# Four banks that keep a tile's attention sums, its new values in one go, and value matmuls on both sides of the transposes

## The chip, the cores and the metric

The kernel runs on one core of a Trainium2 chip. The metric is the device time of one execution in microseconds, lower being better. Before the change it is 2471.74 us, the median of three runs between 2467.19 and 2473.27.

## The reference

Four residual layers are applied one after another to x, which holds 64 batch rows of 32 tokens with 512 features. The time around the change is that of the third layer, attention over a paged cache:

```python
x = x + L0(x)      # per-condition 32x32 mixing of the 32 rows
x = x + L1(x)      # dense 512x512 plus a rank-16 adapter
x = x + L2(x)      # attention, below
x = x + L3(x)      # as L0, other weights

def L2(x):
    q, k, v = x @ Wq.T, x @ Wk.T, x @ Wv.T       # 32 query heads, 8 key/value heads, 128 wide
    q, k = rope(rmsnorm(q, q_norm_w)), rope(rmsnorm(k, k_norm_w))
    k_all = concat(k_cache[block_table], k)      # 512 cached and 32 new keys per batch row
    v_all = concat(v_cache[block_table], v)
    scores = q @ k_all.T * SCALE                 # masked by the cached length
    return (softmax(scores) @ v_all) @ Wo.T
```

All numbers are float32.

## The kernel before

**Tiles, steps, units, slots.** The 2048 tokens form 16 tiles of 128 tokens; a tile holds four batch rows (`NB` = 4). Key/value heads are taken in two groups of four (`KG` = 4), so there are 32 steps of one group and one tile. A step has four units, one for each batch row `j`, and a unit has four heads `k`. One unit and one head make a slot: 512 slots, 16 to a step. Four query heads share a key/value head, so a slot's queries are 4 x 32 = 128 rows.

**What a slot does.** The program order is written out by hand in `slot(i)`, and each engine keeps it. `scores` (L832) multiplies the queries with 544 keys in two matmuls (L838, L841) into a tile of two PSUM banks; VectorE (DVE) adds the mask and takes the row minimum (L846), and ScalarE (ACT) takes the exponential (L857). `divide` (L859) takes the reciprocal of the sum on DVE (L862) and scales on ACT: the 512 cached keys' part (L863) and the 32 new keys' part (L864). Two slots later (`LAG`) `flip` (L877) transposes the 128x512 probabilities with four transposes (L880) into the bank of the tag "t", and DVE copies them out (L882). Three slots later (`VLAG`) `values` (L884) adds four chunks of 128 cached keys into the output sum (L893).

A float32 matmul on TensorE appears in the profile as two passes, a transpose as one.

**New keys.** The 32 new keys of four heads are together 128 rows. `flip_new` (L866) transposes them for a whole unit with one transpose (L873) and ACT copies it out (L875). After the fourth head `values_new` (L901) multiplies each head's 32 rows with the 32 rows of its new values (L905): four small matmuls in four row strips of the array, each into its head's sum. `finish` (L913) then copies the unit's four sums to SBUF with two ACT copies (L919, L922), and after the fourth unit `store` (L927, L929) writes the tile's 1 MB to DRAM, on the SP queue but for the last three steps.

**PSUM.** There are eight banks: two for the scores, one "t", one "m" for projections, three for the sums of heads 0 to 2, and one, "o3", which the sum of head 3 shares in turn with the transposes of the rotated heads (`Norm.turn`, L750) and of the cache pages (`Turn.turn`, L266). ACT copies those transposes out in `keep` (L758, L768, and L278, L283).

**Work beside it.** While attention runs, the next two tiles' projections are made, spread over the slots: one or two halves of a projection matmul in nearly every slot (`project`, L643, L651), DVE additions that combine them (`take`, L667, L663), squares on ACT (`squares`, L702, L707), the power on GpSimd (POOL; `power`, L711), and four norm and rotation pieces on DVE (`scale`, `straight`, `swapped`, `sum`) that `norm_piece` (L950) hands out where a slot has room. The slot after the last piece gets the head's transposes; slots in which head 3's sum is being made are passed over.

**Transfers.** `Unit` loads a unit's 16 key pages from SP (L794), `fetch_values` gathers its four chunks of cached values from POOL (L105), `fetch_new` loads the new values from SP (L816), a slot ahead and with two buffers. After attention, the output products (L1323) and the last mixing follow.

Of the kernel before, what the change touches and what calls it, by code (L numbers as in the profile page):

```python
# [27 lines left out]
F32 = mybir.dt.float32  # L28
# [15 lines left out]
P = 128  # L44
B, S, HID = 64, 32, 512
NT = B * S // P
NB = P // S
NC = HID // P
D = 128
# [28 lines left out]
def resid_kernel(  # L78
# [149 lines left out]
    with ExitStack() as l2:  # L228
# [20 lines left out]
        class Turn:  # L249
# [16 lines left out]
            def turn(self):  # L266
                if self.g:
                    self.ps = room["o"].tile([P, HID], F32, name="pageT_ps", tag="o3")
                else:
                    self.ps = ps_s.tile([P, 2 * HID], F32, name="s_ps")  # L270
                for k in range(KG):
                    nc.tensor.transpose(
                        self.ps[:, k * P : (k + 1) * P],
                        self.rows[:, k // 2, (k % 2) * D : (k % 2 + 1) * D],
                        ident,
                    )
# [420 lines left out]
        class Norm:  # L697
# [52 lines left out]
            def turn(self):  # L750
                if "o" in room:
                    self.tp = room["o"].tile([P, REP, P], F32, name="head_ps", tag="o3")
                else:
                    self.tp = ps_t.tile([P, REP, P], F32, name="head_ps", tag="t")
                for h in range(REP):
                    nc.tensor.transpose(self.tp[:, h, :], self.a[:, h, :], ident)  # L756
# [16 lines left out]
        class Unit:  # L773
# [39 lines left out]
            def fetch_new(self):  # L813

                self.v_new = room["v"].tile([P, D], F32, name="v_new", bufs=2)
                nc.sync.dma_start(  # L816
                    out=self.v_new,
                    in_=vn_dram[self.g][self.t][self.j * S : (self.j + 1) * S, :].rearrange(
                        "s (k d) -> k s d", k=KG
                    ),  # L820
                )

            def begin(self):
# [6 lines left out]
                self.sm, self.total, self.pT, self.o_ps = {}, {}, {}, {}  # L830
# [35 lines left out]
            def flip_new(self):  # L866
# [7 lines left out]
                self.pT_new = room["attn"].tile([P, P], F32, name="pT_new", bufs=1)  # L874
# [9 lines left out]
            def values(self, k):  # L884


                if k == 0:
                    self.o_three = room["o"].tile([P, KG - 1, HID], F32, name="o_ps", tag="o")
                    self.o_ps = {i: self.o_three[:, i, :P] for i in range(KG - 1)}
                elif k == KG - 1:  # L890
                    self.o_ps[k] = room["o"].tile([P, HID], F32, name="o_ps3", tag="o3")[:, :P]
                for c in range(NC):
                    nc.tensor.matmul(  # L893
                        self.o_ps[k],
                        lhsT=self.v[c][:, k * D : (k + 1) * D],
                        rhs=self.pT[k][:, c, :],
                        start=(c == 0),
                        stop=False,
                    )

            def values_new(self):  # L901

                for k in range(KG):
                    rows_k = slice(k * S, (k + 1) * S)
                    nc.tensor.matmul(  # L905
                        self.o_ps[k],
# [3 lines left out]
                        stop=True,  # L910
                    )

            def finish(self):  # L913
                if self.j == 0:
                    oT_of[self.s] = room["attn"].tile([P, KG * REP, P], F32, name="oT", bufs=1)
                dst = oT_of[self.s].rearrange("p (k h) s -> p k h s", k=KG)[
                    :, :, :, self.j * S : (self.j + 1) * S
                ]
                nc.scalar.copy(  # L919
                    dst[:, KG - 1], self.o_ps[KG - 1].rearrange("p (h s) -> p h s", h=REP)  # L920
                )
                nc.scalar.copy(  # L922
                    dst[:, : KG - 1],
                    self.o_three[:, :, :P].rearrange("p k (h s) -> p k h s", h=REP),
                )
# [19 lines left out]
        oT_of, rot_of = {}, {}  # L945
# [4 lines left out]
        def norm_piece(slot):  # L950
# [242 lines left out]
        def slot(i):  # L1193
# [14 lines left out]
            if LAG <= i < n + LAG and (i - LAG) % KG == KG - 1:  # L1208
                turned.flip_new()
            run(i, "turn")  # L1210
            if i >= VLAG:
                old = unit_of[(i - VLAG) // KG]
                old.values((i - VLAG) % KG)
                if (i - VLAG) % KG == KG - 1:
                    old.values_new()
                    at(i, "act", old.finish)
                    if old.j == NB - 1:
                        at(i + 1, "store", old.store)
            if new:
                new.divide(k)  # L1220
# [278 lines left out]
```

## Time and profile before

| | |
|---|---|
| median of three runs | 2471.74 us |
| profiled execution, its own time | 2473.52 us |
| span of that execution | 2471.8 us |
| mean granted TensorE clock | 0.999 |
| busy: PE, DVE, ACT, POOL | 2438.3, 1609.2, 1398.3, 1174.2 us |
| attention slots (from the first to the last scores) | 191.2 to 2078.2 us of the span |
| PE busy in the attention slots | 1878.07 of 1887.00 us |

PE is the matmul engine and PEld its weight loads. A group of instructions is named by its line in the kernel, its engine, its operation, and its tiles as out<-in. In a timeline, neighbouring instructions of one group are one row: where it starts, how long it lasts from its first start to its last end, and how many there are. Matmuls overlap at their ends[...]; so the time that a group takes on TensorE is read from its start to the start of the next group.

### The profile page before, as it was taken

The page shows a single profiled execution, that of the slowest core. Times are in us where ns is not written, and L with a number is a line of the kernel's source. Part 1 is how long each engine was busy: PE and PEld are TensorE (multiplying, and loading weights), DVE is VectorE, ACT ScalarE, POOL GpSimd, SP SyncE. Part 2 cuts the span into 40 slices and gives each one's busy share as a digit, 9 for nine tenths or more (in the row PEclk, how much of TensorE's full clock was granted, in tenths as well). Part 3 has the DMA queues.
Part 4 walks back from the last instruction along what each step waited for, and adds up shares of the span by engine and source line. Part 5 has one row for each costly group of instructions (what it writes and reads, how often), then busy time and mean ns, then how long its engine had stood idle before and what let it go on. Part 6 is the DMA issues. An engine that isn't in the chain of part 4 may idle for free.

```text
span 2471.8 us, 47357 instructions
## 1 busy us (share of the span) xinstructions
PE 2438.3 (99%) x13760; PEld 1855.4 (75%) x13760; DVE 1609.2 (65%) x3602; ACT 1398.3 (57%) x4135; POOL 1174.2 (48%) x1096
## 2 busy tenths in 40 slices
PE   7999999999999999999999999999999999999999
PEld 4556777777777777777777777777777788888887
DVE  5767767676767677777777777777776756433222
ACT  2236767676767767677777777777676754000000
POOL 4436555455555565655556555555555753000000
PEclk9999999999999999999999999999999999999999
DMA  7876666666667677756666666565667784333221
GB/s 237 293 231 199 188 198 191 193 195 189 202 188 209 188 218 220 250 180 194 178 189 176 185 179 186 171 192 173 187 178 220 252 258 155 117 112 129 86 86 60
DMA packets 448545, 459.19 MB, mean 186 GB/s; under 512 B 51424, under 2 KB 379488, under 8 KB 440480
## 3 DMA queue, kind: packets, MB, share of 16 engines
q1 hardware_dynamic: 398384, 291.24, 38.1%
q0 software_dynamic: 49904, 164.93, 22.2%
q8 instruction: 112, 1.84, 0.3%
q14 instruction: 145, 1.19, 0.2%
HBM read 384.66 MB, written 79.69 MB: 188 GB/s over the span
## 4 chain that ended last, share of the span: by engine, by line
PE 95%; DMA 2%; issue 2%; SPq 1%; DVE 0%; POOL 0%; ACT 0%; DVEq 0%; POOLq 0%; ACTq 0%
PE proj_ps L651 23%; PE o_ps L893 18%; PE out_ps L1323 15%; PE s_ps L838 11%; PE s_ps L841 9%; PE pT_ps L880 9%; PE l_ps L490 3%; PE head_ps L756 3%; PE o_ps L905 2%; DMA kT<-kT 1%; PE h_ps L474 1%; SPq L794 1%; PE s_ps L873 1%; PE mix_ps L1341 1%; PE mix_ps L435 1%
## 5 line engine op out<-in xcount | busy, mean ns | idle before, releaser
L105 POOL DMA_INDIRECT v_sb<-v,v_rows x512 | 538.1, 1051 | 352.7 <-PE o_ps L893 242.8
L846 DVE CUSTOM_DVE_ANT_0 sm<-s_ps,pen 128x544 f32<-128x544 f32 x512 | 370.9, 724 | 457.9 <-PE s_ps L841 337.2
L893 PEld LDWEIGHTS o_ps<-pT,v_sb 128*128 128x128 f32 x4096 | 519.2, 192 | 133.6 <-issue 126.3
L857 ACT ACTIVATE sm<-sm,top 128x544 f32<-128x544 f32 x512 | 381.8, 746 | 339.6 <-DVE top L846 266.2
L893 PE MATMUL o_ps<-pT,v_sb 128*128 128x128 f32 x4096 | 541.4, 275 | 2.5 <-issue 1.3
L863 ACT ACTIVATE sm<-sm,share 128x512 f32<-128x512 f32 x512 | 369.8, 722 | 175.9 <-DVE share L862 144.2
L882 DVE COPY pT<-pT_ps 128x512 f32<-128x512 f32 x512 | 351.5, 687 | 8.0 <-PE pT_ps L880 4.1
L838 PE MATMUL s_ps<-kT,qT 128*128 128x288 f32 x1024 | 347.0, 420 | 2.8 <-DMA kT<-kT 2.1
L880 PE MATMUL pT_ps<-ident,sm 128*128 128x128 f32 x2048 | 307.7, 273 | 0.6 <-DVE pT L882 0.6
L841 PE MATMUL s_ps<-kT,qT 128*128 128x256 f32 x1024 | 305.3, 380 | 2.4 <-DMA kT<-kT 2.4
L880 PEld LDWEIGHTS pT_ps<-ident,sm 128*128 128x128 f32 x2048 | 256.1, 141 | 52.5 <-DVE pT L882 1.0
L809 POOL TENSOR_SCALAR pen<-key_f,seq_f 128x544 f32<-128x544 f32 x128 | 285.0, 2227 | 11.6 <-issue 0.3
L712 POOL TENSOR_SCALAR ss<-ss 128x4 f32<-128x4 f32 x160 | 56.4, 353 | 438.1 <-ACT sq L707 437.5
L841 PEld LDWEIGHTS s_ps<-kT,qT 128*128 128x128 f32 x1024 | 194.4, 190 | 57.2 <-issue 2.0
L663 DVE TENSOR_TENSOR raw<-proj_ps,raw 128x512 f32<-128x512 f32 x332 | 223.4, 685 | 18.7 <-PE proj_ps L651 13.9
L707 ACT ACTIVATE sq<-raw 128x128 f32<-128x128 f32 x640 | 197.2, 308 | 18.5 <-DVE raw L663 2.3
L714 POOL TENSOR_TENSOR rstd<-ss,minus_half 128x4 f32<-128x4 f32 x160 | 185.1, 1157 | 13.4
L1373 ACT COPY p<-out_ps 128x256 f32<-128x256 f32 x7 | 2.6, 373 | 333.1 <-PE out_ps L1323 333.1
L651 PE MATMUL proj_ps<-sum,x 128*128 128x512 f32 x380 | 186.9, 594 | 0.0
L105 POOL DMA_INDIRECT mix_rows<-in_w,cond_rows x32 | 33.0, 1031 | 309.3 <-DVE mix_diag L171 299.5
L838 PEld LDWEIGHTS s_ps<-kT,qT 128*128 128x128 f32 x1024 | 154.7, 191 | 20.0 <-issue 3.5
L1323 PE MATMUL out_ps<-w,o_in 128*128 128x256 f32 x768 | 167.1, 379 | 0.0
(175 smaller groups left out, 3492.7 us busy)
## 6 DMA issues: line engine op xcount, KB each, us to landing
kT<-kT SPq DMA_DIRECT2D x2048, 64.0 KB
o<-oT SPq DMA_DIRECT2D x29, 1024.0 KB
o_in<-o SPq DMA_DIRECT2D x28, 1024.0 KB
page_rows<-in_kv_cache SPq DMA_DIRECT2D x32, 256.0 KB
v<-in_kv_cache SPq DMA_DIRECT2D x32, 256.0 KB
kT<-page_rows SPq DMA_DIRECT2D x32, 256.0 KB
vn<-raw SPq DMA_DIRECT2D x32, 256.0 KB
v_sb<-v,v_rows POOLq DMA_INDIRECT x512
```

The lines of the kernel that those rows point to most:

```text
L105: nc.gpsimd.indirect_dma_start(out=dst, out_offset=None, in_=table, in_offset=bass.IndirectOffsetOnAxis(ap=index, axis=0),)
L651: nc.tensor.matmul(self.ps, lhsT=self.pair.x[x][:, c if x == "b" else half.start + c, :], rhs=blocks(self.b)[w][:, c, :], start=(c == 0), ...
L809: nc.gpsimd.tensor_scalar(self.pen, key_f, seq_f[:, self.b : self.b + 1], BIG, ALU.is_ge, ALU.mult)
L838: nc.tensor.matmul(ps[:, first:HID], lhsT=q, rhs=self.kT[:, :n1, k, :], start=True, stop=True)
L841: nc.tensor.matmul(ps[:, HID : first + LA], lhsT=q, rhs=self.kT[:, n1:, k, :], start=True, stop=True)
L846: nc.vector.tensor_tensor_reduce(out=sm, in0=ps[:, first : first + LA], in1=self.pen, scale=1.0, scalar=3e38, op0=ALU.add, op1=ALU.min, ac ...
L857: nc.scalar.activation(sm, sm, AF.Exp, bias=top, scale=-1.0, accum_out=total)
L863: nc.scalar.activation(sm[:, :L], sm[:, :L], AF.Copy, scale=share)
L880: nc.tensor.transpose(ps[:, c, :], self.sm[k][:, c * P : (c + 1) * P], ident)
L882: nc.vector.tensor_copy(pT, ps)
L893: nc.tensor.matmul(self.o_ps[k], lhsT=self.v[c][:, k * D : (k + 1) * D], rhs=self.pT[k][:, c, :], start=(c == 0), stop=False,)
L1323: nc.tensor.matmul(ps[:, :HALF], lhsT=o[:, i, :], rhs=w[i // REP][:, i % REP, :], start=(i == 0), stop=(i == KG * REP - 1),)
```

## The change

The four heads' sums of a whole tile stay in four banks, one for each head, with the four units side by side in 128 columns each; only the first matmul into a bank has the start flag. The new values of the four units are added together after the tile's last slot. Four copies, one for each head, take the sums out, two in that slot and two in the next, and each head's 256 KB is stored by itself, heads 0 and 1 from SP and heads 2 and 3 from POOL. In a slot the value matmuls come right after the scores: two chunks, then the probabilities' transposes, then the other two chunks. `flip_new` and `divide` move ahead of the projections. Head and page transposes use the bank "t". The output buffer `oT` has three parts of a quarter tile, `v_new` and `pT_new` have four buffers, `v_new` is loaded early in its tile, and the cached values are gathered one slot earlier. A diff, cut to its core:

```diff
 # Turn.turn
-                    self.ps = room["o"].tile([P, HID], F32, name="pageT_ps", tag="o3")
+                    self.ps = ps_t.tile([P, HID], F32, name="pageT_ps", tag="t")
 # Norm.turn
-                if "o" in room:
-                    self.tp = room["o"].tile([P, REP, P], F32, name="head_ps", tag="o3")
-                else:
-                    self.tp = ps_t.tile([P, REP, P], F32, name="head_ps", tag="t")
+                self.tp = ps_t.tile([P, REP, P], F32, name="head_ps", tag="t")
 # Unit
-                self.v_new = room["v"].tile([P, D], F32, name="v_new", bufs=2)
+                self.v_new = room["v"].tile([P, D], F32, name="v_new", bufs=NB)
-                self.pT_new = room["attn"].tile([P, P], F32, name="pT_new", bufs=1)
+                self.pT_new = room["attn"].tile([P, P], F32, name="pT_new", bufs=NB)
-            def values(self, k):
-                if k == 0:
-                    self.o_three = room["o"].tile([P, KG - 1, HID], F32, name="o_ps", tag="o")
-                    self.o_ps = {i: self.o_three[:, i, :P] for i in range(KG - 1)}
-                elif k == KG - 1:
-                    self.o_ps[k] = room["o"].tile([P, HID], F32, name="o_ps3", tag="o3")[:, :P]
-                for c in range(NC):
+            def values(self, k, chunks):
+                if self.j == 0 and chunks[0] == 0:
+                    o_of[self.s, k] = room["o"].tile([P, NB, P], F32, name="o_ps", tag=f"o{k}")
+                for c in chunks:
                     nc.tensor.matmul(
-                        self.o_ps[k],
+                        o_of[self.s, k][:, self.j, :],
                         lhsT=self.v[c][:, k * D : (k + 1) * D],
                         rhs=self.pT[k][:, c, :],
-                        start=(c == 0),
+                        start=(self.j == 0 and c == 0),
                         stop=False,
+                        skip_group_check=True,
                     )
 # values_new
-                        self.o_ps[k],
+                        o_of[self.s, k][:, self.j, :],
...
-                        stop=True,
-                    )
-            def finish(self):
-                if self.j == 0:
-                    oT_of[self.s] = room["attn"].tile([P, KG * REP, P], F32, name="oT", bufs=1)
...
-            def store(self):
-                queue = nc.sync if self.s < len(steps) - 3 else nc.gpsimd
-                queue.dma_start(out=o_dram[self.g][self.t], in_=oT_of.pop(self.s))
+                        stop=(self.j == NB - 1),
+                        skip_group_check=True,
+                    )
+        def finish(s, k, copy):
+            o_ps = o_of.pop((s, k))
+            oT = oT_of[s, k] = room["attn"].tile([P, REP, P], F32, name="oT", bufs=3)
+            copy(
+                oT.rearrange("p h (j s) -> p h j s", j=NB),
+                o_ps.rearrange("p j (h s) -> p h j s", h=REP),
+            )
+        def store(s, k):
+            g, t = steps[s]
+            queue = nc.sync if k < 2 and s < len(steps) - 3 else nc.gpsimd
+            queue.dma_start(
+                out=o_dram[g][t][:, k * REP : (k + 1) * REP], in_=oT_of.pop((s, k))
+            )
 # norm_piece
-                while slot in turning or (slot - VLAG) % KG == KG - 1:
+                while slot in turning:
 # the plan of a unit's transfers
-                at(KG * u - 1 + c, "pool", call, unit_of, u, "fetch_values")
-            at(KG * u - 1, "fetch", call, unit_of, u, "fetch_new")
+                at(KG * u - 2 + c, "pool", call, unit_of, u, "fetch_values")
+            at(u // NB * SLOTS + 4 + 3 * (u % NB), "fetch", call, unit_of, u, "fetch_new")
 # slot
                 new.scores(k)
-            if LAG <= i < n + LAG:
-                turned = unit_of[(i - LAG) // KG]
+            old = unit_of[(i - VLAG) // KG] if i >= VLAG else None
+            if old:
+                old.values((i - VLAG) % KG, (0, 1))
+            turned = unit_of[(i - LAG) // KG] if LAG <= i < n + LAG else None
+            if turned:
                 turned.flip((i - LAG) % KG)
+            if old:
+                old.values((i - VLAG) % KG, (2, 3))
+            if turned and (i - LAG) % KG == KG - 1:
+                turned.flip_new()
+            if new:
+                new.divide(k)
+            if old and (i - VLAG) % SLOTS == SLOTS - 1:
+                for u in range(old.u - NB + 1, old.u + 1):
+                    unit_of[u].values_new()
+                for c in range(KG):
+                    last = old.s == len(steps) - 1
+                    copy = nc.vector.tensor_copy if last and c % 2 else nc.scalar.copy
+                    behind = i if last else i + c // 2
+                    at(behind, "out", finish, old.s, c, copy)
+                    at(behind + 1, "store", store, old.s, c)
+            run(i, "out")
             run(i, "pe")
             run(i, "take")
             run(i, "late")
             run(i, "power")
             norm_piece(i)
-            if LAG <= i < n + LAG and (i - LAG) % KG == KG - 1:
-                turned.flip_new()
             run(i, "turn")
-            if i >= VLAG:
-                old = unit_of[(i - VLAG) // KG]
-                old.values((i - VLAG) % KG)
-                if (i - VLAG) % KG == KG - 1:
-                    old.values_new()
-                    at(i, "act", old.finish)
-                    if old.j == NB - 1:
-                        at(i + 1, "store", old.store)
-            if new:
-                new.divide(k)
```

More of the change, by code (lines that the diff above doesn't have):

```diff
@@ L829, in begin @@
                 self.new = room["attn"].tile([P, KG, S], F32, name="p_new")
-                self.sm, self.total, self.pT, self.o_ps = {}, {}, {}, {}
+                self.sm, self.total, self.pT = {}, {}, {}
             def scores(self, k):
@@ L909, in values_new @@
                         start=False,
-                        stop=True,
-                    )
-            def finish(self):
-                if self.j == 0:
-                    oT_of[self.s] = room["attn"].tile([P, KG * REP, P], F32, name="oT", bufs=1)
[L916 to L920, printed above, removed]
-                )
[L922 to L925, printed above, removed]
-            def store(self):
-                queue = nc.sync if self.s < len(steps) - 3 else nc.gpsimd
-                queue.dma_start(out=o_dram[self.g][self.t], in_=oT_of.pop(self.s))
+                        stop=(self.j == NB - 1),
+                        skip_group_check=True,
+                    )
+        def finish(s, k, copy):
[11 more added lines that the diff above has]
+            )
         plan = {}
@@ L944, in resid_kernel @@
         step_of, pair_of, unit_of, turn_of, first_of = {}, {}, {}, {}, {}
-        oT_of, rot_of = {}, {}
+        o_of, oT_of, rot_of = {}, {}, {}
         pieces = []
```

## The prediction

> **What bounds the kernel now.** I read the page first: PE is busy 99% of the span and the chain that ended last is 95% PE. Busy shares of a pipelined engine say little, so I asked for the engines' busy time in two stretches from the middle (columns: stretch, its length, then PE, PEld, DVE, ACT and POOL busy with instruction counts, granted clock, DMA share, GB/s), and then for the timeline of PE alone (columns: start, time, engine, line, operation, count).
>
> ```profile
> PE 95%; DMA 2%; issue 2%; SPq 1%; DVE 0%; POOL 0%; ACT 0%; DVEq 0%; POOLq 0%; ACTq 0%
> ```
>
> ```profile
> 1000.00:1100.00 100.00, 99.80 (x600) 74.71 (x599) 78.22 (x174) 70.79 (x211) 57.60 (x53) 1.00 0.67 207
> 1500.00:1600.00 100.00, 100.00 (x596) 75.29 (x595) 71.10 (x168) 69.06 (x202) 54.10 (x48) 1.00 0.63 186
> ```
>
> ```profile
> 1201.28 1.05 PE L893 MATMUL o_ps<-pT,v_sb 128*128 128x128 f32 x8
> 1202.27 0.50 PE L905 MATMUL o_ps<-pT_new,v_new 32*128 32x128 f32 x8
> 1202.70 0.75 PE L838 MATMUL s_ps<-kT,qT 128*128 128x288 f32 x2
> 1203.29 0.59 PE L841 MATMUL s_ps<-kT,qT 128*128 128x256 f32 x2
> ...
> 1205.02 1.05 PE L893 MATMUL o_ps<-pT,v_sb 128*128 128x128 f32 x8
> 1205.91 0.65 PE L838 MATMUL s_ps<-kT,qT 128*128 128x288 f32 x2
> 1206.40 0.59 PE L841 MATMUL s_ps<-kT,qT 128*128 128x256 f32 x2
> ```
>
> The reader is to see two things. PE has no gap in the attention slots at full clock, so only PE time removed, or a new PE wait, moves the end. And the starts of groups tell what a group really takes. Eight value matmuls followed by scores need 1205.91 - 1205.02 = 0.89 us; followed by L905 they need 1202.27 - 1201.28 = 0.99. L905 itself lasts 0.43 to the next start. The scores after it need 0.59 (1202.70 to 1203.29) where undisturbed ones need 0.49 (1205.91 to 1206.40). So a unit's new values cost 0.10 + 0.43 + 0.10 = 0.63 us, 128 times: 80.6 us of the span. The single records show why: the four passes of the four row strips start within 20 ns, the second passes 214 ns after the first, and the next instruction 200 ns after the last start. A pass of 128 columns elsewhere takes 0.11.
>
> [...] the second pass's record has no exposed load (270 ns, against 372 for the first), and it is in the same strip. [...]
>
> **The change, part by part.** Times are us; S is a slot's first score matmul.
>
> *New values in one go (L905).* The same 1024 matmuls in 32 groups of 32 instead of 128 of 8. I take it that each further pass of a strip costs 0.11 with its load hidden, as between the two passes now. A group then takes 0.43 + 6 x 0.11 = 1.10, with entry and exit 1.30; four groups of now take 4 x 0.63 = 2.52. Gain 1.22 per tile, x32 = **39**. Bounds: if loads in one strip do not hide, six passes cost 0.11 more each, 0.66 per tile, and 18 remain; at best [...] 42.
>
> *Values before and behind the transposes.* No instruction is added; 8 matmuls become 4 and 4 with weight loads hidden as now. Zero on PE. They need pT of the slot before, whose copy (L882) ends about 2.7 after that slot's S; the new place is 3.1 + 0.9 after it or later (2.25 + 0.9 in the one slot of 32 without a projection). Cover 1.3 (0.45), so zero. What it moves: projections start at S + 2.26 instead of S + 1.36, 0.90 later.
>
> *Bank "t".* Head and page transposes now share the bank of pT. A head's copy to SBUF (L768) must end before the next slot's transposes:
>
> ```profile
> 1207.79 0.69 DVE L882 COPY pT<-pT_ps 128x512 f32<-128x512 f32 x1
> 1208.78 0.16 DVE L862 RECIPROCAL share<-total 128x1 f32<-128x1 f32 x1 [0.30 <-ACT sm L857]
> 1208.86 0.69 DVE L663 TENSOR_TENSOR raw<-proj_ps,raw 128x512 f32<-128x512 f32 x1
> ```
>
> ```profile
> 1209.61 0.31 ACT L864 ACTIVATE p_new<-sm,share 128x32 f32<-128x32 f32 x1
> 1209.82 0.56 ACT L768 COPY qT<-head_ps 128x512 f32<-128x512 f32 x1
> 1210.28 0.31 ACT L707 ACTIVATE sq<-raw 128x128 f32<-128x128 f32 x1
> ...
> 1211.90 0.73 ACT L857 ACTIVATE sm<-sm,top 128x544 f32<-128x544 f32 x1
> ```
>
> Next S is 1209.46. The copy ends at 1210.38; the new transposes want the bank at 1209.46 + 0.93 + 0.45 = 1210.84. Slack 0.46, set by ACT's order; the head's transposes, now last in the slot, end early enough for that (about 1209.8 with the time that a result takes to reach ACT). So zero in an ordinary slot, with 0.46 to spare.
>
> *Reciprocal (L862) ahead of the take and the first norm piece on DVE.* It waits for ACT's exp, and what queues behind it on DVE are the norm pieces and takes (L663). The lines show where it pinches: the squares (L707, four pairs, 1210.28 to about 1211.9) already hold the next exp up by some 0.5. Five of the ten squares of two tiles follow a slot with two projections, whose take now ends 0.9 later; squares, exp and reciprocal slip, and DVE stands where it used to do a norm piece. Walking the fullest stretch (the last four slots of two tiles' blocks) by these durations: the scores reduction is 0.5 late in the slot without a projection, only 2.25 long once its new values are gone, and PE waits 0.3 for it; the next slot's head transposes wait 0.25 for pT; 0.05 more follows. That is 0.6 per two tiles, x16 = **+10**. Bounds: 0 (one 0.2 less at each step) and 27 (0.2 more, and the stretches after the other two-projection slots too).
>
> *Finishing.* ACT has now 128 x (0.257 + 0.481) = 94 us of copies at L919 and L922; later 126 of 128x512, by the nearest row (L768) 0.564, 71 us, and two on DVE. A tile's sums leave in two slots, before the bank is wanted by 0.8 or more: zero. The fourth oT tile waits for the store of the first; SP issues a tile's store now 0.85 to 1.2 after S of the slot after, the fourth copy falls due near S + 4. Landing of this store isn't shown; kT's in the chain took 2.62. Zero, at most 0.3 a tile if it lands late (10). At the end four copies in two engines stand ahead of the output products (0.77 now): **+1**.
>
> *Queues.* SP gets one store more per tile (0.34 each), POOL two (0.60, by L929's three there), 40 us on an engine 48% busy; behind them are gathers and the norm powers, needed one slot or more later. The v_new loads come earlier and SP's 165.8 us of waiting for L905 mostly goes, off the path. Value gathers are issued one slot earlier: the waits view has 1.2 for a gather and 1.3 of issue at L893, and 1.0 at L873 for the reduction, which the new order gives more time: **-2**. If POOL falls a slot behind instead, no gain here.
>
> **Sum** against the profiled execution's 2473.5: -39 + 10 + 1 - 2 = -30, 2443.5. That execution lay 1.8 above the median 2471.7, so I expect **2442**.
>
> **Rivals.** *A, as summed* (0.75): 2430 to 2452. *B, the passes in a strip don't overlap their loads* (0.08): -18 - 2 + 1 and about +7 of waits, 2460; [...] against it the 270 ns second pass. *C, ACT and DVE set the pace in the full stretches* (0.12): waits of 25 to 40 us eat most of the gain: -39 - 2 + 1 + 25 to 40, so 2457 to 2472; for it DVE's 78% in one stretch, against it that no wait shows there now. *D, slower* (0.05): the one bank "t" stalls PE in every slot with a head or page transposes, 160 + 16 of them. With 0.4 lost in each, +70, so 2471.7 - 30 + 70 = 2512. It decides from the point where the copy ends on average 0.46 + 30/176 = 0.63 later than now. Against it is the ACT order above. [...]
>
> **How the numbers follow.** About 0.3% (7.4 us) is what a measurement of this kernel can tell from no change. A, B and half of C (to 2464) lie beyond it: 0.90 faster; the rest of C 0.05 same; D 0.05 slower. Range 2430 (full 42, no waits) to 2460 (27 of waits, or B).
>
> **What would show it.** PE timeline: one L905 group of 32 in 16 slots, 1.1 long, entry and exit 0.10 each; 1.3 or more means B. No L905 elsewhere, and scores after values 0.49. Waits view: PE or PEld at pT_ps L880 for ACT's L768 near zero; much of it is D. PE at the scores, or head_ps for DVE's pT, some 10 us. PE busy per slot-stretch a little below 100. Wrong: waits above 25 us, or a group that takes 2 us.

## The result, and the profile after

The changed kernel takes **2458.23 us** (median of 8 runs, 2455.69 to 2460.12), against 2472.1 for the kernel before on the same chip (8 runs, 2467.19 to 2480.43): a ratio of 0.9945, 95% interval 0.9931 to 0.9958. It is faster, by 14 us; the forecast was 30. The profiled execution has a span of 2457.8, 14.0 less than before, at a mean granted clock of 0.996 where before had 0.999.

In the page's chain of work that ended last, PE has 93% (95 before), and ACT and DVE, at 0% before, have a share:

```profile
PE 93%; DMA 2%; ACT 2%; DVE 1%; issue 1%; SPq 1%; POOL 0%; ACTq 0%; DVEq 0%; POOLq 0%
```

The same two stretches of the middle follow, in the columns that the prediction names. In one of them PE is now idle for 1.4 us, where it had 0.2:

```profile
1000.00:1100.00 100.00, 98.60 (x613) 76.16 (x612) 79.33 (x170) 72.42 (x211) 57.58 (x57) 1.00 0.70 207
1500.00:1600.00 100.00, 99.97 (x583) 76.28 (x582) 74.64 (x166) 72.02 (x213) 57.23 (x56) 1.00 0.63 182
```

PE's timeline shows the new slot, and the one group of new values of a tile (L900):

```profile
1204.19 0.65 PE L835 MATMUL s_ps<-kT,qT 128*128 128x288 f32 x2
1204.68 0.59 PE L838 MATMUL s_ps<-kT,qT 128*128 128x256 f32 x2
1205.11 0.61 PE L887 MATMUL o_ps<-pT,v_sb 128*128 128x128 f32 x4
1205.56 0.60 PE L877 MATMUL pT_ps<-ident,sm 128*128 128x128 f32 x4
1205.99 0.61 PE L887 MATMUL o_ps<-pT,v_sb 128*128 128x128 f32 x4
1206.53 1.17 PE L900 MATMUL o_ps<-pT_new,v_new 32*128 32x128 f32 x32
1207.63 1.13 PE L651 MATMUL proj_ps<-sum,x_b 128*128 128x512 f32 x2
1208.60 0.65 PE L835 MATMUL s_ps<-kT,qT 128*128 128x288 f32 x2
```

From start to start: the four value matmuls ahead of the group take 0.54 (0.45 where transposes follow), the group 1.10 (1206.53 to 1207.63), and the two projection passes behind it 0.97 where 0.86 is usual. So entry costs about 0.10, the group 1.10 and exit about 0.10, as forecast.

**Where the 14 us come from.** I cut both spans at the first scores of a slot. The differences (after less before) are: up to the first scores +0.9, slots 0 to 31 +0.7, slots 32 to 511 -22.6, from the last scores to the end +7.0. In a stretch of 26 whole tiles (400 to 1950 us of the span) I then added up, for each step of PE from the start of one group to the start of the next, what it takes beyond its usual value; call that the excess. The new values cost 65.7 us there before and 33.9 after. That is 0.632 a unit before and 1.30 a tile now, so 1.22 gained a tile, and **39.1** for 32. All other excess was 2.4 before and is 15.8 now: 13.4 more, **16.5** for 32 tiles. So -39.1 + 16.5 = -22.6 in the slots, and +7.0 and +1.6 at the ends: -14.0.

**The waits in the slots.** Of the 15.8 us, 4.8 stand ahead of the probabilities' transposes, and 2.1 between them (in the late step shown below the four transposes take 0.49 to the next group, 1036.13 to 1036.62, where 0.43 is usual). Another 3.4 stand ahead of the head transposes, 1.3 between them, and 2.5 ahead of `flip_new`. The largest single one is in ACT's timeline, and then in PE's:

```profile
1033.72 0.56 ACT L913 COPY oT<-o_ps 128x512 f32<-128x512 f32 x1
1035.00 0.59 ACT L913 COPY oT<-o_ps 128x512 f32<-128x512 f32 x1 [0.72 <-DMA o<-oT]
1035.48 0.59 ACT L765 COPY qT<-head_ps 128x512 f32<-128x512 f32 x1
```

```profile
1034.38 0.61 PE L887 MATMUL o_ps<-pT,v_sb 128*128 128x128 f32 x4
1036.13 0.66 PE L877 MATMUL pT_ps<-ident,sm 128*128 128x128 f32 x4 [1.14 <-ACT qT L765]
```

The reader sees a chain of three. A tile's fourth copy waits for a store to free its buffer; the copy of a rotated head out of bank "t" stands behind it on ACT; the transposes want bank "t". Such a wait for a store is rare: 4 times in the 26 tiles, 2.8 us on ACT. PE's step from 1034.38 is 1.75 instead of 0.45.

**The tail.** DVE's timeline after the last scores, and what PE does there; PE's row of before is the last:

```profile
2066.39 0.69 DVE L913 COPY oT<-o_ps 128x512 f32<-128x512 f32 x1 [2.38 <-PE o_ps L900]
2067.18 3.50 DVE L1319 TENSOR_TENSOR w<-wo 128x1024 f32<-128x1024 f32 x3
2070.60 0.68 DVE L913 COPY oT<-o_ps 128x512 f32<-128x512 f32 x1
```

```profile
2071.43 9.39 PE L1324 MATMUL out_ps<-wo,o_in 128*128 128x256 f32 x32 [4.47 <-DVE oT L913]
```

```profile
2087.69 7.17 PE L1323 MATMUL out_ps<-wo,o_in 128*128 128x256 f32 x32 [0.77 <-ACT oT L922]
```

The last tile's fourth copy comes 3.5 us late, behind three sums of output weights; PE waits 4.47 for it where it waited 0.77 before. Then 32 output matmuls take 9.39, and took 7.17 before. The eighth column of the engines' busy time by stretches, the granted clock (one before the DMA share), says why:

```profile
2066.00:2069.00 3.00, 0.96 (x14) 0.43 (x10) 2.51 (x3) 1.35 (x3) 1.69 (x3) 1.00 0.21 86
2069.00:2072.00 3.00, 0.57 (x2) 0.52 (x3) 3.00 (x4) 0.00 (x0) 0.43 (x1) 0.52 0.49 176
2072.00:2075.00 3.00, 3.00 (x9) 2.37 (x8) 0.41 (x1) 0.00 (x0) 0.11 (x1) 0.50 0.25 93
2075.00:2078.00 3.00, 3.00 (x13) 2.59 (x12) 0.00 (x0) 0.00 (x0) 1.36 (x3) 0.84 0.38 103
```

The clock falls to 0.50 during the gap, at 2069.1, and stays there for 6.8 us, some 2.3 of which are still the gap.

**The start.** POOL's timeline around the first scores, PE's second scores, and the clock. The two rows of before follow them:

```profile
192.48 1.12 POOL L105 DMA_INDIRECT v_sb<-v,v_rows  x1 [2.27 <-DMA kT<-kT]
193.68 0.22 POOL L712 TENSOR_SCALAR ss<-ss 128x4 f32<-128x4 f32 x1
193.98 1.05 POOL L714 TENSOR_TENSOR rstd<-ss,minus_half 128x4 f32<-128x4 f32 x1
195.13 2.12 POOL L806 TENSOR_SCALAR pen<-key_f,seq_f 128x544 f32<-128x544 f32 x1
```

```profile
198.07 0.80 PE L835 MATMUL s_ps<-kT,qT 128*128 128x288 f32 x2 [3.84 <-DVE top L843]
```

```profile
199.00:202.00 3.00, 3.00 (x8) 1.67 (x7) 2.09 (x7) 1.78 (x4) 2.61 (x3) 0.50 0.69 183
```

```profile
191.45 2.12 POOL L809 TENSOR_SCALAR pen<-key_f,seq_f 128x544 f32<-128x544 f32 x1
194.39 0.75 PE L838 MATMUL s_ps<-kT,qT 128*128 128x288 f32 x2 [0.71 <-issue]
```

The first unit's gather, issued a slot earlier than before, waits 2.27 us for a load, and the first mask (L806; L809 before, where it starts at 191.45) waits behind it until 195.13. DVE needs that mask, PE needs DVE: a gap of 3.84 (0.71 before), and again a clock of 0.50, from 198.6 to 202.1.

### The profile page after: what moved, and what is told of

Its sections match the earlier page's. It is cut to its first block, busy times and chain, and to the rows that moved or that the text cites. A ratio compares the mean times of both kernels' runs of the same rounds, so it can differ in the third digit from the quotient of the medians.

```text
span 2457.8 us, 47106 instructions
## 1 busy us (share of the span) xinstructions
PE 2413.1 (98%) x13760; PEld 1866.2 (76%) x13760; DVE 1675.9 (68%) x3604; ACT 1397.4 (57%) x4005; POOL 1187.5 (48%) x1163
## 4 chain that ended last, share of the span: by engine, by line
PE 93%; DMA 2%; ACT 2%; DVE 1%; issue 1%; SPq 1%; POOL 0%; ACTq 0%; DVEq 0%; POOLq 0%
PE proj_ps L651 22%; PE o_ps L887 17%; PE out_ps L1324 15%; PE s_ps L835 10%; PE pT_ps L877 9%; PE s_ps L838 8%; PE l_ps L490 3%; PE head_ps L753 3%; PE o_ps L900 1%; DMA o<-oT 1%; PE s_ps L870 1%; PE h_ps L474 1%; PE proj_ps L1145 1%; SPq L791 1%; DMA kT<-kT 1%
## 5 line engine op out<-in xcount | busy, mean ns | idle before, releaser
L105 POOL DMA_INDIRECT v_sb<-v,v_rows x512 | 545.3, 1065 | 364.3 <-PE o_ps L887 248.8
L887 PE MATMUL o_ps<-pT,v_sb 128*128 128x128 f32 x4096 | 623.6, 275 | 0.0
L887 PEld LDWEIGHTS o_ps<-pT,v_sb 128*128 128x128 f32 x4096 | 577.8, 191 | 27.0 <-DVE pT L879 0.5
L835 PE MATMUL s_ps<-kT,qT 128*128 128x288 f32 x1024 | 334.2, 408 | 5.6 <-DVE top L843 3.8
L835 PEld LDWEIGHTS s_ps<-kT,qT 128*128 128x128 f32 x1024 | 179.2, 190 | 152.2 <-issue 127.2
L806 POOL TENSOR_SCALAR pen<-key_f,seq_f 128x544 f32<-128x544 f32 x128 | 284.7, 2224 | 11.4
L877 PEld LDWEIGHTS pT_ps<-ident,sm 128*128 128x128 f32 x2048 | 238.6, 141 | 9.1 <-ACT qT L765 6.0
L838 PEld LDWEIGHTS s_ps<-kT,qT 128*128 128x128 f32 x1024 | 194.4, 190 | 57.9 <-ACT p_new L861 3.8
L859 DVE RECIPROCAL share<-total 128x1 f32<-128x1 f32 x512 | 83.6, 163 | 177.8 <-ACT sm L854 163.3
L712 POOL TENSOR_SCALAR ss<-ss 128x4 f32<-128x4 f32 x160 | 40.3, 252 | 325.6 <-ACT sq L707 322.1
L714 POOL TENSOR_TENSOR rstd<-ss,minus_half 128x4 f32<-128x4 f32 x160 | 167.3, 1046 | 13.3
```

The costliest lines, as they stand in the source:

```text
L105: nc.gpsimd.indirect_dma_start(out=dst, out_offset=None, in_=table, in_offset=bass.IndirectOffsetOnAxis(ap=index, axis=0),)
L806: nc.gpsimd.tensor_scalar(self.pen, key_f, seq_f[:, self.b : self.b + 1], BIG, ALU.is_ge, ALU.mult)
L835: nc.tensor.matmul(ps[:, first:HID], lhsT=q, rhs=self.kT[:, :n1, k, :], start=True, stop=True)
L838: nc.tensor.matmul(ps[:, HID : first + LA], lhsT=q, rhs=self.kT[:, n1:, k, :], start=True, stop=True)
L877: nc.tensor.transpose(ps[:, c, :], self.sm[k][:, c * P : (c + 1) * P], ident)
L887: nc.tensor.matmul(o_of[self.s, k][:, self.j, :], lhsT=self.v[c][:, k * D : (k + 1) * D], rhs=self.pT[k][:, c, :], start=(self.j == 0 and ...
```

## The experiments

Times in us; the ratio is to the kernel before on the same chip. e1 to e4 ran on one chip, e5 to e8 on a second and e9 to e11 on a third, where before takes 2473.6, 2474.9 and 2471.3. A difference of two medians below also carries what the chips differ by, up to 3.6 us; so stretches of single profiles are read beside it.

| run | median | ratio, 95% interval |
|---|---|---|
| after | 2458.23 | 0.9945 (0.9931 to 0.9958) |
| e1_per_unit | 2494.71 | 1.0088 (1.0073 to 1.0104) |
| e2_mask_first | 2453.06 | 0.9917 (0.9903 to 0.9931) |
| e3_tail_buffer | 2449.26 | 0.9905 (0.9890 to 0.9920) |
| e4_divide_late | 2448.45 | 0.9903 (0.9888 to 0.9918) |
| e5_three_repairs | 2450.88 | 0.9906 (0.9888 to 0.9923) |
| e6_projections_between | 2460.48 | 0.9940 (0.9927 to 0.9952) |
| e7_old_order | 2535.95 | 1.0249 (1.0233 to 1.0266) |
| e8_values_behind | 2471.80 | 0.9987 (0.9979 to 0.9995) |
| e9_two_repairs | 2448.68 | 0.9912 (0.9895 to 0.9929) |
| e10_out_first | 2444.32 | 0.9883 (0.9867 to 0.9900) |
| e11_tail_and_division | 2441.71 | 0.9875 (0.9859 to 0.9892) |

My theory after the result: the group of 32 gives what was forecast, and four new waits take it back (the tail, the start, the early division, bank "t"). The rival: the new order of the slot or the four banks cost PE time everywhere.

**The new values alone (e1).** The kernel after, with the new values added after each unit again:

```diff
+            if old and (i - VLAG) % KG == KG - 1:
+                old.values_new()
             if old and (i - VLAG) % SLOTS == SLOTS - 1:
-                for u in range(old.u - NB + 1, old.u + 1):
-                    unit_of[u].values_new()
```

> The changed kernel, but each unit's new values are added right after its own fourth head (128 groups of 8 passes, as before the change); all else stays. Theory: the change of array mode is the gain, 1.18 us per tile by the traces, 38 us in all; undoing it adds 38 us, of which the in-slot waits that stand there now (some 15 us) may hide up to 10: 2486 to 2496, with PE groups of 0.43 and 0.10 lost on each side again. Rival: the one long group gains little and the smaller number of copies and stores is what helped: under 2468.

Measured: 2494.71, 36.5 more than after. PE's timeline of e1 shows the old price:

```profile
1209.05 0.61 PE L887 MATMUL o_ps<-pT,v_sb 128*128 128x128 f32 x4
1209.59 0.50 PE L900 MATMUL o_ps<-pT_new,v_new 32*128 32x128 f32 x8
1210.02 1.98 PE L651 MATMUL proj_ps<-sum,x 128*128 128x512 f32 x4
```

The entry is 0.10 and the group 0.43 again, 128 times. The gain of the one go is shown, and so is that the rest of the change by itself costs about 21 (2494.7 against 2473.6 for before).

**The tail's buffer (e3).** The last tile's fourth copy gets a buffer that is free by then:

```diff
-            oT = oT_of[s, k] = room["attn"].tile([P, REP, P], F32, name="oT", bufs=3)
+            if s == len(steps) - 1 and k == KG - 1:
+                oT = oT_of[s, k] = room["attn"].tile([P, REP, P], F32, name="oT3", tag="pT")
+            else:
+                oT = ... # as before
```

> The changed kernel, but the fourth copy of the last tile goes into a probability buffer that is free by then, so it waits for no store. Theory: the fourth oT tile waits for the first one's store, three weight sums slip ahead of it on DVE, and PE stands 4.63 us before the output products, followed by 6.8 us at half clock: the gap falls to about 1.3 and the half clock goes, 3.3 + 3.4 = 6.7 us less, 2451.5. Rival: the copies themselves set the gap (two in a row on ACT and on DVE) and the half clock is chance: 0 to 2 less, 2456 to 2458.

Measured: 2449.26, 9.0 less than after. In DVE's timeline of e3 the two copies now stand together, ahead of all the weight sums, and PE starts after 0.87 for another engine and takes 7.14 for its 32:

```profile
2060.11 1.29 DVE L916 COPY oT<-o_ps 128x512 f32<-128x512 f32 x2 [2.38 <-PE o_ps L900]
2061.31 4.62 DVE L1322 TENSOR_TENSOR w<-wo 128x1024 f32<-128x1024 f32 x4
```

```profile
2061.54 7.14 PE L1327 MATMUL out_ps<-wo,o_in 128*128 128x256 f32 x32 [0.87 <-ACT p L1160]
```

From the last scores to the end of the last matmul it is 390.65 us in e3, e5, e9, e10 and e11, which have this edit, against 396.5 in after (395.9 in e2 and e4, where half clock lasts 3.4 and not 6.8 us) and 389.6 in before. So 5.85 of the tail's 7.0 was the buffer: 3.6 of wait and 2.25 of half clock. The other 3 us of the median are not in the tail; they belong to the spread described below.

**The first mask (e2).**

```diff
-            at(KG * (u - 1) + 1 if u else -1, "pool", call, unit_of, u, "mask")
+            at(KG * (u - 1) + 1 if u else -2, "pool", call, unit_of, u, "mask")
```

> The changed kernel with the first unit's mask one slot earlier, ahead of the first gather on POOL. Theory: the 3.84 us wait of the second slot's scores comes from the first mask, queued behind a gather that waits for stored values, and the half clock of 3.4 us that follows belongs to it: both go, 3.3 + 1.7 = 5 us less, 2453. Rival: the first slots are held up by key pages or by the ACT table load anyway, and the half clock is chance: 0 to 2 us less, 2456 to 2458.

Measured: 2453.06, 5.2 less. The mask and PE's second scores in e2:

```profile
190.20 2.45 POOL L806 TENSOR_SCALAR pen<-key_f,seq_f 128x544 f32<-128x544 f32 x1 [1.28 <-DMA kT<-kT]
193.47 0.75 PE L835 MATMUL s_ps<-kT,qT 128*128 128x288 f32 x2 [0.25 <-DVE top L843]
```

The mask starts at 190.20, the scores wait 0.25, and the clock stays at 1.00. Slots 0 to 31 take 117.1, 118.5, 116.8 and 116.5 in the profiles of e2, e9, e5 and e10, which have this edit, and 119.7, 119.8, 119.2 and 120.1 in after, e3, e4 and e11, which don't. So 2.5 on average is its own.

**The late division (e4).** The division, and the finishing copies with it, move behind the first norm piece:

```diff
-            if new:
-                new.divide(k)
...
-            run(i, "out")
             run(i, "pe")
...
             norm_piece(i)
+            if new:
+                new.divide(k)
+            run(i, "out")
             run(i, "turn")
```

> The changed kernel with the reciprocal and the two scalings behind the projections and the first norm piece again, as before the change; PE's order is that of the changed kernel. Theory P: DVE standing at the reciprocal, which now precedes the norm piece, makes most of the 15 us of in-slot waits in the middle: 8 to 12 us less, 2446 to 2450, DVE's wait for ACT's exp falls from 163 us to under 100. Rival Q: the projections, and with them the takes and squares, come 0.9 us later in a slot, and the place of the reciprocal matters little: within 3 us of 2458. Rival R: ACT then gets its shares later and the head copies are late in bank t: 5 us more or worse.

Measured: 2448.45, 9.8 less. By stretches it is in the slots: slots 32 to 479 take 1634.2 in e4 and 1635.7 in e11, which has the same edit, against 1642.9 to 1644.1 in after, e2, e3 and e9. That is 9.9 and 8.4 less than after. DVE's wait at the reciprocal for ACT's exponential falls from 163.3 us to 66.1 over the whole run. In the waits of 400 to 1950 us (us, times, longest), PE's weight loads wait less for DVE's copy of pT; after's row first, then e4's:

```profile
PEld head_ps L753 <- DVE pT L879: 49.0, 122, 0.9
```

```profile
PEld head_ps L753 <- DVE pT L879: 33.1, 111, 1.0
```

Of these 49.0 and 33.1 us only a part is lost PE time. Counted from start to start, the waits of after ahead of head transposes (3.4) and `flip_new` (2.5) fall to 1.0 and 0.9 here; those ahead of the probabilities' transposes fall only from 4.8 to 4.1. The reciprocal did hold DVE, as forecast; what is left ahead of the probabilities' transposes has another cause.

**Three repairs together (e5).** The edits of e2, e3 and e4.

> The changed kernel with the three edits of the runs before together: first mask ahead of the first gather, fourth copy of the last tile in a free buffer, reciprocal and scalings behind the first norm piece. Theory: the three losses lie in different places (start, end, middle slots) and add up: 2458.2 - 5.2 - 9.0 - 9.8 = 2434, 38 under before, which is the gain of the mode switches alone. Rival: they overlap, through the half clock or through slack that one gives the other: 2440 to 2446.

Measured: 2450.88. The gains did not add. ACT's timeline shows a new wait where two of the tile's copies are made, and PE's the price:

```profile
1143.03 0.31 ACT L861 ACTIVATE p_new<-sm,share 128x32 f32<-128x32 f32 x1
1144.93 1.07 ACT L916 COPY oT<-o_ps 128x512 f32<-128x512 f32 x2 [1.59 <-PE proj_ps L651]
```

```profile
1144.27 0.65 PE L835 MATMUL s_ps<-kT,qT 128*128 128x288 f32 x2
1144.76 0.59 PE L838 MATMUL s_ps<-kT,qT 128*128 128x256 f32 x2
1145.57 0.71 PE L887 MATMUL o_ps<-pT,v_sb 128*128 128x128 f32 x4 [0.22 <-ACT oT L916]
```

The copies wait for the slot's projections, 16.8 us in 11 waits from 400 to 1950 us, and the next tile's first values wait for the copies: the step after the scores is 0.81 instead of 0.43. That slot of every other step is 0.39 longer on average than in after, which makes 5.5 in the 14 such slots of slots 32 to 479. In ACT's timeline of e4 the same copies, in the same place of the order, follow the scaling at once:

```profile
1141.97 0.31 ACT L861 ACTIVATE p_new<-sm,share 128x32 f32<-128x32 f32 x1
1142.18 1.05 ACT L913 COPY oT<-o_ps 128x512 f32<-128x512 f32 x2
```

Three more runs looked for the pair that collides.

**Tail and mask (e9).** The edits of e2 and e3.

> The kernel after with two repairs that touch only its ends: the first unit's mask one slot earlier, and a buffer of its own for the last tile's fourth copy. Theory (the losses at the start and at the tail are separate, each a wait of PE near 4 us with a stretch at half clock behind it): the single gains of 5.2 and 9.0 add, 2458.2 - 14.2 = 2444. Rival (single gains are partly the same noise of alignment, and do not add, as three repairs did not): 2449 or more.

Measured: 2448.68, the rival's number. But both edits still act: the tail is 390.65 long, and slots 0 to 31 take 1.2 less than in after (2.7 in e2).

**Tail and division (e11).** The edits of e3 and e4.

> The buffer for the last copy and the late division (with the copies behind it), the first mask left where it is. It tells which pair does not add. If the three repairs failed by the mask's shift, this one gives 2458.2 - 9.0 - 9.8 = 2439; if the tail's buffer brings the copy's wait for the projections into the middle, it gives 2450 or more, with ACT waits at the finishing copy for PE proj_ps in the trace.

Measured: 2441.71, the best of all. These two add, and there is no wait of a copy for projections. So the tail's buffer did not bring that wait.

**All three, the copies ahead of the projections (e10).** As e5, with `run(i, "out")` left where after has it.

> The three repairs together, but the finishing copies stand where the kernel after has them, ahead of the slot's projections, and only the division stands behind the first norm piece. Theory (three repairs together lost what the late division gives because ACT's finishing copy waited for the projections, 18 us in 12 waits, and PE's next values for the copy): the wait is gone, and the three gains of 5.2, 9.0 and 9.8 add: 2434, at most 2438. Rival (the late division itself collides with something, or ACT's copy now stands ahead of the scalings and delays the exp): 2445 to 2452.

Measured: 2444.32. But for one wait of 3.3 us, no copy waits for projections. Slots 32 to 255 and 288 to 447 are 4.2 and 3.6 shorter than in after, nearly what e4 has there (5.0 and 3.8). Slots 256 to 287, between them, are 2.7 longer: a copy waits 1.85 for a store, PE then waits 1.92 for bank "t", and a clock of 0.50 follows. In all of slots 32 to 479 e10 gains 6.2 where e4 gains 9.9. So the division alone, without the copies' move, makes most of e4's gain.

The 2434 I expected did not come, since the singles' gains were overrated. By their own stretches they are 2.5, 5.85 and 9.9, together 18 and not 24. That gives 2440 for three, which lies in e10's interval (0.9867 to 0.9900 of 2471.31: 2438 to 2447); 2442.5 for e11 (measured 2441.7); and 2449.9 for e9 (2448.7). e5 lacks about 11 to its 2440: 5.5 are the copies' wait above, and 4.0 stand in slots 480 to 511.

The rest is spread. Slots 480 to 511, which no edit aims at, take from 98.2 (e2) to 105.3 (e5) in the profiles of after, e2 to e5 and e9 to e11; 101.3 in after and 104.0 in before. PE waits there for loads of keys or for a late copy out of bank "t", 1 to 3 us at a time and at other places in each, and some of these waits have a clock of 0.50 behind them. In e11:

```profile
1997.35 0.65 PE L835 MATMUL s_ps<-kT,qT 128*128 128x288 f32 x2
2000.29 1.03 PE L838 MATMUL s_ps<-kT,qT 128*128 128x256 f32 x2 [2.30 <-DMA kT<-kT]
2001.12 1.06 PE L887 MATMUL o_ps<-pT,v_sb 128*128 128x128 f32 x4
```

The scores take 1.03 after a wait of 2.30, the values 1.06, where 0.59 and 0.61 are usual; the clock from 2002 to 2004 is 0.53.

The copies' wait shows where two edits stand together, the mask's and the move of the copies behind the projections. e8 and e6 below have both and long waits at the copies too (19.5 us in 11 for projections, 18.1 in 12 for the new values). e4 and e11, with the copies moved and the mask left, have none; e7, with another order of the slot, has waits of its own. How a mask at the very start changes what a copy waits for in the middle stays open.

**The order of the slot.** The kernel after, without any of the three repairs, keeps bank "t" and the one go but takes the order of before: transposes, projections, first norm piece, `flip_new`, head transposes, then all four chunks of values and the division.

```diff
-            if old:
-                old.values((i - VLAG) % KG, (0, 1))
...
                 turned.flip((i - LAG) % KG)
-            if old:
-                old.values((i - VLAG) % KG, (2, 3))
+            run(i, "pe")
...
             run(i, "turn")
+            if old:
+                old.values((i - VLAG) % KG, (0, 1, 2, 3))
```

> The new values in one go, four banks and bank t as in the changed kernel, but a slot in the order of before: transposes, projections, transpose of new keys, head transposes, then all four value chunks, then the reciprocal. Theory: bank t forces the order: head transposes come 0.86 us after the probabilities' transposes and must wait for DVE's copy out of the bank, some 0.4 us in each of about 130 slots with one projection, and gain is lost: 40 to 60 us more than with the repaired order, 2480 to 2510, with PE waiting at head_ps for DVE's pT. Rival: the copy is out in time, the reciprocal is late as before, and the order of before is as good: 2445 to 2450.

Measured: 2535.95, 78 more than after and more than I expected. From 400 to 1950 us, steps into head transposes cost 43.6 us more than undisturbed, and 66 of them come behind a projection with 0.5 us each. The row of the waits, to be held against after's 49.0 in 122 above:

```profile
PEld head_ps L753 <- DVE pT L879: 86.5, 106, 2.6
```

The head transposes need the bank that DVE is still copying pT out of, 106 times. So with one bank for both, the order of before is not usable; rival D's mechanism exists, and the change's order avoids most of it.

**All values behind the transposes (e8).** As e5, with the first two chunks moved behind:

```diff
-            if old:
-                old.values((i - VLAG) % KG, (0, 1))
...
-                old.values((i - VLAG) % KG, (2, 3))
+                old.values((i - VLAG) % KG, (0, 1, 2, 3))
```

> As the kernel with the three repairs, but all four value chunks stand behind the probabilities' transposes. Theory: the transposes come 0.45 us earlier and the 0.46 us of slack that a head copy has in bank t is gone: in 176 slots PE waits 0 to 0.3 us at the transposes for ACT's copy, 15 to 40 us more than with the repairs. Rival: the head transposes end early enough that ACT's copy is out, and the halves bring nothing: within 4 us of the repaired kernel.

Measured: 2471.80, 21 more than e5 on the same chip. The transposes now come 0.45 earlier, and wait for ACT's copy of the heads. After's row in the waits of 400 to 1950 us, then e8's:

```profile
PEld pT_ps L877 <- ACT qT L765: 3.8, 6, 1.3
```

```profile
PEld pT_ps L877 <- ACT qT L765: 28.9, 79, 1.9
```

From start to start, 118 steps from scores to transposes lose 21.7 us here. Two chunks ahead of the transposes are what keeps bank "t" off the path in most slots.

**Projections between (e6).** As e5, with the projections between the transposes and the second half of the values, outside the slots of `flip_new`:

```diff
                 turned.flip((i - LAG) % KG)
+            mid = i >= VLAG and (i - LAG) % KG != KG - 1
+            if mid:
+                run(i, "pe")
             if old:
```

> As the kernel with the three repairs, and in the slots without a transpose of new keys the projections stand between the probabilities' transposes and the second half of the values, 0.45 us earlier than in the changed kernel. Theory: takes, squares and exps come earlier and what is left of in-slot waits in the middle (some 7 us, most of them at the transposes for ACT's head copy) falls: 2 to 5 us less than with the three repairs. Rival: what is left comes from bank t alone, which this doesn't touch: no change within 2 us. Below zero: the take is early but the transposes of heads are not, and the slots with a new-key transpose fall behind: 2 more.

Measured: 2460.48, about 10 more than e5 on the same chip; I had expected 2 to 5 less. In the profiled execution, the slowest of the five, waits ahead of the probabilities' transposes double (10.1 us from 400 to 1950, against 5.3 in e5), and more come at the scores (6.7 against 0.8).

## Why the prediction was wrong

The forecast was -30 on the profiled execution; it was -14. The gain was right. What failed are three terms that were put at nothing or nearly so: the end (+1, measured +7.0), bank "t" in the slots (0, measured over 6), and POOL's queue at the first unit (0, measured 2.5). By the prediction's own steps:

- **New values in one go, -39: right.** Measured 39.1, with entry, group and exit at 0.10, 1.10 and 0.10 as forecast. By the prediction's estimate the group would have been 0.66 longer if each of its six further passes had paid for its own load (rival B). The trace shows nothing of it: two passes in a strip took 0.43 and eight take 1.10, which is 0.11 for each further one, as for a pass elsewhere.
- **Values split around the transposes, 0; four banks, 0: right as to PE's own time.** The usual value of each step is the same in both traces (0.49 and 0.43 for the scores, 0.43 to 0.44 for four transposes, 0.86 for two projection passes), which answers the rival above; e8 shows that the split is needed.
- **Reciprocal ahead of the norm piece, +10, and gathers, -2: about as priced, in part at another place.** Slots lost 16.5 net where 8 was in the sum. e4, e11 and e10 take 9.9, 8.4 and 6.2 of it off by moving the division, so the term has the size that was given. Of the two places named for it, the head transposes did wait (3.4 us and 1.3 between them); the scores, meant to wait 0.3 at a time, lost 0.0 in 264 steps behind projections. `flip_new`, which was to gain, lost 2.5.
- **Bank "t", 0 with 0.46 to spare: the step that failed in the slots.** After e4's edit, waits ahead of the probabilities' transposes remain (4.1 us, and 1.0 between the four, in 26 tiles; over 6 for all 32). I took the slack from one ordinary slot. In after, about half of the loss at these transposes (3.4 of 6.9 us) lies in the two slots right after the copies of a tile. ACT is late there, and now and then one of the copies waits for a store. "Zero, at most 0.3 a tile" was priced as ACT's own delay, and bank "t" behind it was not considered. No run frees bank "t" by itself, so this rests on the traces and on how much e8 lost with 0.45 less of slack. The rest, in other slots of a step, I did not trace further.
- **The end, +1: the largest miss, 7.0.** I counted the copies' own time, not the buffer. There are three buffers, the fourth copy needs the first store to be done, and three weight sums of 3.5 us together stand ahead of it on DVE. I had named that very wait for the ordinary tiles ("the fourth oT tile waits for the store of the first") and not asked for it at the one place where nothing covers it. e3 gives 5.85 back.
- **POOL's queue, "needed one slot or more later": wrong for the first unit.** The mask of the first unit stood behind the earlier gather. It cost 2.5 (e2), and with it slots 0 to 31 come out at +0.7 rather than a gain; the +0.9 up to the first scores is spread (189.5 to 192.1 in the profiles of after, e1 to e6 and e8 to e11).
- **Half clock after a gap: not in the sum.** It made about 2.25 of the loss at the tail (9.39 for the output matmuls against 7.14 in e3), and at the start an estimated 1.7, half of the 3.4 us at a clock of 0.50. In after, gaps of 3.84 and 4.47 were followed by a clock of 0.50; a gap of 1.92 in e10 was too, and one of 3.13 in e7 was not. The last section has the measure that fits. Before has one such stretch itself, of 3.4 us at 2003.7, behind waits of 0.79 and 1.47 for keys, so "no gap in the attention slots at full clock" was not quite so.

Together the misses are 8.5 in the slots, 6.0 at the end and 1.6 at the start: 16. That 2458 still lies between 2430 and 2460 is luck: the upper end stood for 27 us of waits through the reciprocal, which cost 6 to 10, and the rest came from terms that were at nothing or nearly so. Rivals B and D did not come. C has the right size of effect in the wrong form: ACT and DVE do not set a pace; single waits, most of them under 0.5 us and the longest 1.3, stand in a few slots of each tile. With the tail's buffer and the late division, e11 takes 2441.7.

## What to carry to other kernels

When an edit packs work to save changes between 128-row and 32-row matmuls (0.20 us for each group here), its gain can be read from single records in advance. What it changes beside that (a bank shared, a buffer fewer, a queue reordered) must be walked through at the slots after a tile's end and at the first and last tile, not in an ordinary slot. A wait named as covered needs its cover named at the start and the end too, where there is none. When single repairs are to add, read each one's gain from the stretch it touches, since the medians here carried some us of unrelated spread (slots 480 to 511 alone took from 98.2 to 105.3).

## What the runs showed of the hardware

**What brings half clock.** The length of a gap alone does not tell: in e10 a gap of 1.92 us (from 1146.8) was followed by half clock and one of 2.12 (from 912.2) was not; nor was one of 3.13 in e7. In all thirteen traces the granted clock changed only on a fixed grid of 3.41 us (in after, between 150 and 2110 us, at 198.6, 202.1, 2069.1 and 2076.0). Cut along that grid, PE's busy time (third column) and the clock (eighth) in e10 are:

```profile
910.78:914.19 3.41, 1.42 (x9) 1.08 (x7) 1.41 (x4) 3.18 (x9) 2.42 (x3) 1.00 1.05 357
914.19:917.61 3.42, 3.29 (x16) 2.23 (x17) 1.08 (x3) 2.00 (x6) 1.25 (x1) 1.00 0.51 164
1146.30:1149.71 3.41, 1.49 (x14) 1.30 (x13) 1.02 (x3) 2.63 (x6) 1.65 (x3) 1.00 0.77 246
1149.71:1153.12 3.41, 3.41 (x8) 1.93 (x7) 2.01 (x5) 0.93 (x2) 2.04 (x1) 0.50 0.69 204
```

These two lie at the edge. Between 150 and 2110 us of all thirteen traces, every one of the 17 grid stretches at full clock in which PE was busy less than 41.5% was followed by one at half clock (in after and before they are three, with PE busy 0.57, 1.24 and 1.14 of 3.41 us); of 16 between 41.5 and 55%, 3 were; of over 7000 above that, none. A half-clock stretch was followed by another where PE was busy less than 78% of it (6 of 6), and by full clock where it was busy 93% or more (20 of 20). So in the tail of after, where PE was busy for 1.11 us of the first, it took 6.8 us, and in e2 and e4 3.4. With PE busy throughout, a stretch of 3.4 us at a clock of 0.50 costs an estimated 1.7.

**Changing between 128-row and 32-row matmuls** cost 0.10 on the way in and 0.10 on the way out, whether the group between had 8 passes (before: 0.99 against 0.89 for eight value matmuls, then 0.59 against 0.49 for the scores) or 32 (after: 0.54 against 0.45 for four, then 0.97 against 0.86 for the projection).
